# One-hot sort comparisons of a graph kernel, regrouped from alternating three-column units to whole pieces of six columns

## Chip, cores and metric

The kernel runs on one core of one Trainium2 chip. The metric is device time in microseconds (us) of one execution. The kernel before was run three times: 1296.0, 1299.63 and 1299.84 us, median 1299.63 us.

## What is computed

A residual graph layer on 6250 nodes and 206,250 edges of 128 float32 features. The edges' features are added up by the node that `src` names, the sum goes with `x` and one global vector through a small network, and the result is normalised:

```
edge_aggr = zeros((n, 128)).at[src].add(edge_attr_128)
combined = concat([x, edge_aggr, global_expand], -1) @ W_c + b_c
h = softplus(combined @ W1 + b1)
h = softplus(h @ W2 + b2)
x = layernorm(x + h @ W3 + b3)
```

Nearly all the time goes into the first line: the nodes are in no order that the core could use, so the kernel sorts the edges by node range itself.

## The kernel before, in words

The 6250 nodes are cut into 32 buckets of 196. The edges lie as 1692 columns of 122 edges, one edge per partition. Two columns make a pair (846 pairs), three pairs make a **piece** (`pieces`, L1094), and the pairs belong to eight groups of 28 to 128 pairs. A group whose number of pairs is no multiple of three ends in a smaller piece.

Five kinds of work run at once through one long stretch, each on an engine of its own:

- **Positions** (L445 to L760, VectorE with small matmuls on TensorE): for each coming group, in which place of a column each edge lands when the column is sorted by bucket (`slot`), and where the sorted pairs go in memory (`pair`). The tiles `pair_ib`, `past`, `hi_of` and `sum_of` belong to it. Groups 5 to 7 go through the counting twice; their first passes are laid into the time of groups 2 to 4.
- **Comparison** (`compare`, L1124): for each column a one-hot matrix `sort_hot`, 122 edges by 128 places, which says where each edge goes. VectorE does it by one equality of `slot` with a row of numbers. ScalarE does it in two steps: per column an `Abs` of the difference (L1140, the column's `slot` being its bias operand), then one `Relu` of 1 minus that (L1142), whose bias operand is a column of the tile `ones`.
- **Gather** (`gather`, L1145, TensorE): one float32 matmul per column, one-hot by edge rows, into a PSUM bank of a pool of three. The profile counts each such matmul twice.
- **Settle** (`settle`, L1157, ScalarE): two copies per three columns from the bank into one of six `pairs` tiles (sets 108 to 113), one tile for each piece.
- **Scatter** (`scatter_row`, L1176, GpSimd): one indirect DMA per pair writes its 128 rows to scratch memory (`rows_by`), 846 in all.

Rows that have been scattered are loaded back as `chunks` (L920), compared with the node numbers of a bucket on VectorE (`match`, tile `hot`, L983), multiplied on TensorE (`product`, L1006) and added up on VectorE (`add`, tile `sums_t`, L1029). What is still left of these sums when the last pair has been scattered is done together with the node network (`node_layers`, L1334), which ends the kernel. ScalarE also writes the bucket codes behind each load of edge rows (`code_rows`, L1105), and `log1p` (L1359) is a step of the softplus.

**Units before.** A piece of three pairs is two units of three columns (`units`, L1117), first the columns of even number (n = 0), then the odd ones (n = 1). By `(2 * i + n) % SHARE` with `SHARE` 2, each piece has its even unit compared on VectorE and its odd unit on ScalarE, there as three `Abs` and one `Relu` in a row. The comparison of a unit has a tile of its own, from a pool of five.

**What sets the order.** TensorE, VectorE, ScalarE and SyncE carry out their instructions in an order written by hand. Every step is entered with a planned time (`when`, L1248), all are sorted by it (L1325) and issued in that order; the planned times do nothing else. A scatter is planned every `SCATTER` = 1.3 us. With t the planned time of a piece's first scatter, its even unit is compared at t - 17.5, gathered at t - 14.0, settled at t - 10.5; its odd unit comes 1.95 us later in each (L1264 to L1266).

Of the kernel before, what the change touches and what calls it, by code (L numbers as in the profile page):

```python
# [7 lines left out]
F32 = mybir.dt.float32  # L8
# [5 lines left out]
AF = mybir.ActivationFunctionType  # L14
ALU = mybir.AluOpType
# [3 lines left out]
P = 128  # L19
# [18 lines left out]
PN = 122  # L38
# [4 lines left out]
PAIRS = 3  # L43
THREE = 3
# [15 lines left out]
SCATTER = 1.3  # L60
LOADED, CODED, COMPARED, GATHERED, SETTLED = 36.0, 21.0, 17.5, 14.0, 10.5
FIRST = 24.0
SOON, FLAGGED = 4.0, 15.9
SHARE = 2
PREP, LAG = 0.85, 11.0
TOGETHER, BEHIND = 2, 1
AT_END, FIRST_STEPS = 4, 9
# [74 lines left out]
def kernel(  # L142
# [21 lines left out]
    nc = tc.nc  # L164
# [15 lines left out]
    groups = []  # L180
# [74 lines left out]
    ones = const.tile([P, P], F32, name="ones")  # L255
# [57 lines left out]

    with ExitStack() as phase:
        rows_p = phase.enter_context(tc.tile_pool(name="rows", bufs=ROWS))
        sort_p = phase.enter_context(tc.tile_pool(name="sort", bufs=5))
        pairs_in = phase.enter_context(tc.tile_pool(name="pairs_in", bufs=2))
        per = phase.enter_context(tc.tile_pool(name="per", bufs=2))
        keep = phase.enter_context(tc.tile_pool(name="keep", bufs=1))
# [3 lines left out]
        iota_ps, slot_ps, twice_ps = (both_ps[:, a:a + w] for a, w in (  # L323
            (0, BL), (2 * P, P), (3 * P, P // 2)))
# [8 lines left out]
        dump, by_slot, bucket_of, quad_of, twice, half_p, before_f, awaited = (  # L333
            of_plain[n] for n in ("dump", "by_slot", "bucket_of", "quad_of", "twice", "half_p",
                                  "before", "awaited"))
# [106 lines left out]
        slot_of, pair_of, ends_of = {}, {}, ([0.0, 0.0], [0.0, 0.0])  # L442
        slots_done, pairs_done = set(), set()
# [615 lines left out]
        def node_rows():  # L1059
# [16 lines left out]
            def biases():  # L1076
# [17 lines left out]
        pieces = [(g, t, min(PAIRS, s1 - t)) for g, (s0, s1) in enumerate(groups)  # L1094
                  for t in range(s0, s1, PAIRS)]
# [9 lines left out]
        def code_rows(i):  # L1105
            a, b = LOAD_COLS * i, min(LOAD_COLS * (i + 1), NC)
            nc.scalar.copy(rows_at[i][:PN, :b - a, D:W], pair_low[:, a:b].unsqueeze(2))  # L1107
# [9 lines left out]
        def units(i):  # L1117

            k = pieces[i][2]
            return [(i, lo, min(THREE, k - lo), n) for lo in range(0, k, THREE) for n in range(2)]  # L1120

        hot_of, sorted_of = {}, {}

        def compare(unit):  # L1124
            i, lo, m, n = unit
            g, c, _ = pieces[i]
            slot = slot_of[g]
            assert all((g, 2 * (c - groups[g][0] + lo + j) + n) in slots_done for j in range(m))
            hot = sort_p.tile([P, THREE, P], F32, name="sort_hot")
            hot_of[unit] = hot  # L1130
            if (2 * i + n) % SHARE == 0:
                at = 2 * (c - groups[g][0] + lo) + n
                nc.vector.tensor_tensor(  # L1133
                    hot[:PN, :m],
                    slot[:PN, at:at + 2 * m - 1:2].unsqueeze(2).to_broadcast([PN, m, P]),
                    slot_ps[:PN].unsqueeze(1).to_broadcast([PN, m, P]), op=ALU.is_equal)
                return
            for j in range(m):
                at = 2 * (c - groups[g][0] + lo + j) + n
                nc.scalar.activation(hot[:PN, j], by_slot[:PN], AF.Abs,  # L1140
                                     bias=slot[:PN, at:at + 1], scale=-1.0)
            nc.scalar.activation(hot[:PN, :m], hot[:PN, :m], AF.Relu, bias=ones[:PN, :1],  # L1142
                                 scale=-1.0)

        def gather(unit):  # L1145
            i, lo, m, n = unit
            hot = hot_of.pop(unit)
            out = opened_bank(lambda: settle(unit))
            sorted_of[unit] = out
            for j in range(m):  # L1150
                at = 2 * (lo + j) + n
                col = 2 * pieces[i][1] + at
                nc.tensor.matmul(out[:, j, :], hot[:PN, j],  # L1153
                                 rows_at[col // LOAD_COLS][:PN, col % LOAD_COLS, :],
                                 start=True, stop=True)

# [37 lines left out]
        with tc.manual_schedule(engines={ET.PE, ET.DVE, ET.Activation, ET.SP}):  # L1194
# [53 lines left out]
            def when(t, step):  # L1248
                events.append((t, len(events), step))
# [5 lines left out]
            for i, t in enumerate(first_at):  # L1255
                if t >= LOADED:
                    when(t - LOADED, lambda i=i: load_rows(i))
                when(t - CODED, lambda i=i: code_rows(i))
            for i, t in enumerate(begins):
                mine = units(i)  # L1260
                for u, unit in enumerate(mine):
                    late_by = SCATTER * pieces[i][2] * u / len(mine)
                    soon = 0.0 if i or u else SOON
                    when(t - COMPARED + late_by - soon, lambda unit=unit: compare(unit))  # L1264
                    when(t - GATHERED + late_by - 1.7 * soon, lambda unit=unit: gather(unit))
                    when(t - SETTLED + late_by, lambda unit=unit: settle(unit))  # L1266
            for t, i, j in at_time:
# [66 lines left out]
    def node_layers(sums, ready):  # L1334
# [23 lines left out]

        def log1p(layer, n0, w):  # L1359
            away = sub_z[layer, n0][1]  # L1360
            nc.scalar.activation(away[:, :w], away[:, :w], AF.Ln, bias=ones[:, :1])

        def softplus(layer, n0, w):

# [240 lines left out]
```

## Time and profile before

The profile is of one execution on the chip. That execution took 1298.25 us, of which the span from the first to the last instruction is 1296.5 us; 1.75 us lie around it. It is 1.38 us under the median of the three runs.

| | before |
|---|---|
| median of three runs | 1299.63 us |
| the profiled execution, and its span | 1298.25 us, 1296.5 us |
| TensorE matmuls busy | 1169.6 us (90%) |
| VectorE (DVE) busy | 1073.4 us (83%), 2403 instructions |
| ScalarE (ACT) busy | 1064.2 us (82%), 2484 instructions |
| GpSimd (POOL) busy | 877.7 us (68%), 915 instructions |
| mean granted TensorE clock | 0.963 |
| mean DMA traffic | 295 GB/s |
| first scatter, last scatter begin | 23.39 us, 1132.43 us |

The profile names PE (TensorE), DVE (VectorE), ACT (ScalarE), POOL (GpSimd) and SP (SyncE), and lines as L1140, the line of the program. A group's row gives the line, engine and operation, what is written and read, the number of instructions, then busy time and mean length of one, then the idle time of the engine just before them and what ended it. A timeline row gives start, length and instruction; its bracket is idle time before it with what ended that. In the chain of waits a row is a start, a duration and what the time went to. Two float32 instructions in a row can overlap at their ends, so several together can take less than their lengths added up.

### The profile page before, as it was taken

Reading aid. Unit: us, or ns where it says so; the run is one execution under the profiler, and the core shown is the slowest. Engines: PE = TensorE matmul, PEld = TensorE weight load, DVE = VectorE, ACT = ScalarE, POOL = GpSimd, SP = SyncE. Lnnn points to the kernel's source line nnn. Section 1 sums busy time; section 2 is a strip of 40 time slices with the busy share of each in tenths; the row PEclk is TensorE's granted clock in tenths of the full one; section 3 lists DMA queues with packets and bytes.
Section 4 is the critical chain, followed back from the end, with each engine's and each line's share of the span. In section 5 each row is a group of like instructions: output and inputs, shape, how many; then the busy total and the mean of one; then the engine's idle time right before and its main releaser. Section 6 shows DMA issues by size and latency. Waiting matters only on the chain.

```text
span 1296.5 us, 26618 instructions
## 1 busy us (share of the span) xinstructions
PE 1169.6 (90%) x8617; PEld 1108.0 (85%) x8617; DVE 1073.4 (83%) x2403; ACT 1064.2 (82%) x2484; POOL 877.7 (68%) x915
## 2 busy tenths in 40 slices
PE   5767898878999998999899999999999999999893
PEld 4657788877998898998799999999999999998762
DVE  7968988998899988899878887799877666687784
ACT  5998998899978898987999999998999999504353
POOL 2777777777776677776777777777777777740334
PEclk9888998989999899999999999999999999999996
DMA  6789998899999998996989999999999999874421
GB/s 227 245 273 346 344 326 305 305 337 369 364 321 316 362 329 295 311 316 238 314 296 306 325 332 321 355 294 325 337 348 336 361 340 353 279 220 144 142 77 52
DMA packets 174638, 381.99 MB, mean 295 GB/s; under 512 B 27546, under 2 KB 118626, under 8 KB 160670
## 3 DMA queue, kind: packets, MB, share of 16 engines
q1 hardware_dynamic: 130751, 260.70, 60.4%
q0 software_dynamic: 41328, 115.65, 23.0%
q10 hardware_dynamic: 2415, 3.87, 0.8%
q8 instruction: 72, 1.18, 0.4%
q14 instruction: 72, 0.59, 0.1%
HBM read 242.49 MB, written 142.20 MB: 297 GB/s over the span
## 4 chain that ended last, share of the span: by engine, by line
PE 42%; DVE 21%; DMA 15%; ACT 9%; issue 7%; POOL 6%; SPq 0%; ACTq 0%; DVEq 0%; POOLq 0%
PE part L1006 24%; PE sorted L1153 13%; DMA rows_by<-pairs,pair 11%; POOL rows_by L1182 6%; ACT pairs L1165 6%; DVE hot L983 4%; DMA chunks<-rows_by 3%; ACT sort_hot L1140 2%; DVE sort_hot L1133 2%; DVE pair_ib L491 2%; DVE past L720 2%; DVE sums_t L1029 2%; DVE slot L569 1%; PE small L1383 1%; DMA rows<-in_edge 1%
## 5 line engine op out<-in xcount | busy, mean ns | idle before, releaser
L1182 POOL DMA_INDIRECT rows_by<-pairs,pair x846 | 824.8, 975 | 306.9 <-issue 204.5
L1006 PE MATMUL part<-hot,chunks 128*128 128x196 f32 x3516 | 674.1, 335 | 12.2 <-DVE sums_t L1029 9.2
L1165 ACT COPY pairs<-sorted 64x387 f32<-64x387 f32 (+2 forms) x1144 | 542.7, 474 | 70.0 <-PE sorted L1153 49.5
L1006 PEld LDWEIGHTS part<-hot,chunks 128*128 128x128 f32 x3516 | 581.1, 192 | 21.2 <-DVE sums_t L1029 10.3
L1153 PE MATMUL sorted<-rows,sort_hot 122*128 122x129 f32 x3384 | 497.4, 287 | 43.3 <-ACT pairs L1165 37.2
L1153 PEld LDWEIGHTS sorted<-rows,sort_hot 122*128 122x128 f32 x3384 | 454.0, 198 | 55.6 <-ACT pairs L1165 51.8
L983 DVE TENSOR_TENSOR hot<-chunks,both_ps 128x784 f32<-128x784 f32 (+3 forms) x541 | 427.9, 810 | 5.6 <-DMA chunks<-rows_by 5.2
L1140 ACT ACTIVATE sort_hot<-plain,slot 122x128 f32<-122x128 f32 x846 | 278.3, 391 | 13.1 <-DVE slot L569 7.1
L1029 DVE TENSOR_TENSOR sums_t<-sums_t,part 128x392 f32<-128x392 f32 (+1 forms) x262 | 143.5, 548 | 117.4 <-PE part L1006 116.7
L1142 ACT ACTIVATE sort_hot<-sort_hot,ones 122x384 f32<-122x384 f32 (+2 forms) x286 | 174.6, 611 | 9.3
L1133 DVE TENSOR_TENSOR sort_hot<-slot,both_ps 122x384 f32<-122x384 f32 (+2 forms) x286 | 154.5, 541 | 3.2 <-PE sorted L1153 3.0
L491 DVE TENSOR_TENSOR pair_ib<-pair_block,both_ps 122x512 bf16<-122x512 bf16 (+2 forms) x157 | 103.5, 664 | 0.3
L1425 POOL TENSOR_SCALAR y<-y,mv,rs 128x128 f32<-128x128 f32 x40 | 31.1, 785 | 96.9 <-issue 67.7
L569 DVE TENSOR_REDUCE slot<-small 122x16 f32<-122x512 f32 (+2 forms) x109 | 72.8, 668 | 15.3 <-PE small L552 14.8
L1355 ACT ACTIVATE away<-sorted,z_bias 128x512 f32<-128x512 f32 (+2 forms) x13 | 8.5, 656 | 70.8 <-DMA chunks<-rows_by 46.3
L550 PE MATMUL small<-pair_ib,half 122*122 122x512 bf16 (+2 forms) x109 | 43.0, 395 | 10.0 <-DVE slot L569 9.6
L735 PEld LDWEIGHTS <-past 128*128 128x128 f16 x424 | 24.9, 99 | 17.9 <-DVE past L720 12.6
L720 DVE TENSOR_TENSOR past<-both_ps,starts 128x512 f16<-128x512 f32 (+1 forms) x61 | 40.0, 666 | 0.3
L735 PE MATMUL small<-jump,past 128*128 128x56 f16 (+3 forms) x424 | 29.2, 190 | 11.5 <-DVE past L720 8.1
L1107 ACT COPY rows<-pair_i 122x16 f32<-122x16 f32 x106 | 22.6, 213 | 17.8 <-DMA rows<-in_edge 16.9
L552 PEld LDWEIGHTS <-starts_h 128*122 128x122 bf16 x236 | 24.9, 146 | 12.1 <-issue 7.6
L720 DVE TENSOR_TENSOR past<-both_ps,starts_late 128x512 f16<-128x512 f32 (+2 forms) x49 | 32.3, 661 | 0.0
(163 smaller groups left out, 520.0 us busy)
## 6 DMA issues: line engine op xcount, KB each, us to landing
rows<-in_edge SPq DMA_DIRECT2D x105, 1032.0 KB
chunks<-rows_by SPq DMA_DIRECT2D x362, 136.0 KB
chunks<-rows_by SPq DMA_DIRECT2D x203, 204.0 KB
chunks<-rows_by SPq DMA_DIRECT2D x75, 272.0 KB
rows_by<-pairs,pair POOLq DMA_INDIRECT x846
rows_by<-fill SPq DMA_DIRECT2D x10, 1249.5 KB
rows_by<-fill SPq DMA_DIRECT2D x10, 714.0 KB
chunks<-rows_by SPq DMA_DIRECT2D x13, 408.0 KB
```

The source lines that it names most:

```text
L491: nc.vector.tensor_tensor(ib, pair_block[:, cols].unsqueeze(2).to_broadcast([PN, n, SB]), iota_ps[:PN, :SB].unsqueeze(1).to_broadcast([PN, ...
L569: nc.vector.tensor_reduce(to, of, axis=mybir.AxisListType.X, op=ALU.max)
L720: nc.vector.tensor_tensor(past[:, :, a:b], twice_ps[:KB].unsqueeze(1).unsqueeze(1).to_broadcast([KB, 2, b - a, P // 2]), own["starts"][:, ...
L983: nc.vector.tensor_tensor(hot[:, q - a:q - a + m], chunks[j][:, lo:hi + 1:step, D:W].to_broadcast([P, m, BL]), iota_ps.unsqueeze(1).to_bro ...
L1006: nc.tensor.matmul(part[:, b - base_of[v], :], t[:, place_in(j, q), :D], hot[:, q - a], start=first, stop=last)
L1029: nc.vector.tensor_add(here, here, of)
L1133: nc.vector.tensor_tensor(hot[:PN, :m], slot[:PN, at:at + 2 * m - 1:2].unsqueeze(2).to_broadcast([PN, m, P]), slot_ps[:PN].unsqueeze(1).to ...
L1140: nc.scalar.activation(hot[:PN, j], by_slot[:PN], AF.Abs, bias=slot[:PN, at:at + 1], scale=-1.0)
L1142: nc.scalar.activation(hot[:PN, :m], hot[:PN, :m], AF.Relu, bias=ones[:PN, :1], scale=-1.0)
L1153: nc.tensor.matmul(out[:, j, :], hot[:PN, j], rows_at[col // LOAD_COLS][:PN, col % LOAD_COLS, :], start=True, stop=True)
L1165: nc.scalar.copy(sets_at[i][64 * n:64 * n + 64, lo:lo + m, h, :W], out[64 * h:64 * h + 64, :m, :])
L1182: s = nc.gpsimd.indirect_dma_start(out=dst, out_offset=bass.IndirectOffsetOnAxis(ap=at, axis=0), in_=rows[:, j].rearrange("p a b -> p (a b ...
```

## The change

`compare` works by piece. A piece of even number is compared whole on VectorE, in one instruction of six columns (122x768 for a full piece). A piece of odd number is compared whole on ScalarE: six `Abs`, one per column in column order, and one `Relu` over all six. `Relu` (and the `Ln` in `log1p`) gets its 1 as a number in the instruction instead of a column of `ones`. The tile pool `sort` has three tiles of six columns where it had five of three. The ScalarE steps of a piece are entered one by one, starting at t - 19.5 and 0.65 us apart (`SPREAD`, `SCATTER / 2`), so that the seventh, the `Relu`, has t - 15.6; the VectorE step stays at t - 17.5. Gathers, settles, scatters and all else keep their planned times.

```diff
-SHARE = 2
+SHARE, SPREAD = 2, 2.0
...
-        sort_p = phase.enter_context(tc.tile_pool(name="sort", bufs=5))
+        sort_p = phase.enter_context(tc.tile_pool(name="sort", bufs=3))
...
-            hot = sort_p.tile([P, THREE, P], F32, name="sort_hot")
-            hot_of[unit] = hot
-            if (2 * i + n) % SHARE == 0:
...
-            nc.scalar.activation(hot[:PN, :m], hot[:PN, :m], AF.Relu, bias=ones[:PN, :1],
-                                 scale=-1.0)
+            hot = hot_of[i] = sort_p.tile([P, 2 * PAIRS, P], F32, name="sort_hot")
+            if i % SHARE == 0:
+                return [lambda: nc.vector.tensor_tensor(
+                    hot[:PN, :2 * m], slot[:PN, at:at + 2 * m].unsqueeze(2).to_broadcast([PN, 2 * m, P]),
+                    slot_ps[:PN].unsqueeze(1).to_broadcast([PN, 2 * m, P]), op=ALU.is_equal)]
+            return [lambda j=j: nc.scalar.activation(
+                hot[:PN, j], by_slot[:PN], AF.Abs, bias=slot[:PN, at + j:at + j + 1], scale=-1.0)
+                for j in range(2 * m)] + [lambda: nc.scalar.activation(
+                    hot[:PN, :2 * m], hot[:PN, :2 * m], AF.Relu, bias=1.0, scale=-1.0)]
...
-                nc.tensor.matmul(out[:, j, :], hot[:PN, j],
+                nc.tensor.matmul(out[:, j, :], hot[:PN, at],
...
+                if i % SHARE == 0:
+                    when(t - COMPARED - soon, lambda i=i: compare_next(i))
+                else:
+                    for j in range(2 * pieces[i][2] + 1):
+                        when(t - COMPARED - SPREAD + j * SCATTER / 2, lambda i=i: compare_next(i))
...
-                    when(t - COMPARED + late_by - soon, lambda unit=unit: compare(unit))
...
-            nc.scalar.activation(away[:, :w], away[:, :w], AF.Ln, bias=ones[:, :1])
+            nc.scalar.activation(away[:, :w], away[:, :w], AF.Ln, bias=1.0)
```

`compare_next(i)` issues the next of a piece's steps. What stands on TensorE, GpSimd and SyncE, and in which order, is the same as before. On VectorE and ScalarE it changes.

ScalarE in the second group, before: the copies of piece 28 (set 112, even number) and piece 29 (set 113, odd number) and what stands around them.

```order
L1140 ACTIVATE sort_hot<-plain,slot 122x128 x3
L1142 ACTIVATE sort_hot<-sort_hot,ones 122x384
L1165 COPY pairs_112<-sorted 64x3x129 x4
L1140 ACTIVATE sort_hot<-plain,slot 122x128 x3
L1142 ACTIVATE sort_hot<-sort_hot,ones 122x384
L1165 COPY pairs_113<-sorted 64x3x129 x4
```

ScalarE at the same place now, from the last `Abs` of piece 29 to the `Relu` of piece 31.

```order
L1133 ACTIVATE sort_hot<-plain,slot 122x128
L1135 ACTIVATE sort_hot<-sort_hot 122x768
L1158 COPY pairs_112<-sorted 64x3x129 x4
L1133 ACTIVATE sort_hot<-plain,slot 122x128 x2
L1158 COPY pairs_113<-sorted 64x3x129 x2
L1133 ACTIVATE sort_hot<-plain,slot 122x128 x3
L1158 COPY pairs_113<-sorted 64x3x129 x2
L1133 ACTIVATE sort_hot<-plain,slot 122x128
L1135 ACTIVATE sort_hot<-sort_hot 122x768
```

Six `Abs` of two runs of three stand now in runs of two, three and one, between the two pairs of copies of a ScalarE piece, and one `Relu` of 768 stands for two of 384.

VectorE in the fifth group (while pairs 348 to 471 are scattered), before, with the two comparisons of two neighbouring pieces:

```order
L983 TENSOR_TENSOR hot<-chunks,both_ps 128x784
L1133 TENSOR_TENSOR sort_hot<-slot,both_ps 122x384
L491 TENSOR_TENSOR pair_ib<-pair_block,both_ps 122x512
L720 TENSOR_TENSOR past<-both_ps,starts_late 128x512
L569 TENSOR_REDUCE slot<-small 122x2x2x4
L1029 TENSOR_TENSOR sums_t<-sums_t,part 128x392
L491 TENSOR_TENSOR pair_ib<-pair_block,both_ps 122x512
L1133 TENSOR_TENSOR sort_hot<-slot,both_ps 122x384
L720 TENSOR_TENSOR past<-both_ps,starts_late 128x512
L983 TENSOR_TENSOR hot<-chunks,both_ps 128x784 x2
```

VectorE at the same place now:

```order
L983 TENSOR_TENSOR hot<-chunks,both_ps 128x784
L491 TENSOR_TENSOR pair_ib<-pair_block,both_ps 122x512
L720 TENSOR_TENSOR past<-both_ps,starts_late 128x512
L569 TENSOR_REDUCE slot<-small 122x2x2x4
L1029 TENSOR_TENSOR sums_t<-sums_t,part 128x392
L491 TENSOR_TENSOR pair_ib<-pair_block,both_ps 122x512
L1130 TENSOR_TENSOR sort_hot<-slot,both_ps 122x768
L720 TENSOR_TENSOR past<-both_ps,starts_late 128x512
L983 TENSOR_TENSOR hot<-chunks,both_ps 128x784 x2
```

The comparison of the odd-numbered piece is gone from VectorE; that of the even-numbered one has twice the columns, at the place of its first unit.

VectorE at the start of the program, before, where the first pieces are compared between the position steps of the first group:

```order
L1133 TENSOR_TENSOR sort_hot<-slot,both_ps 122x384
L720 TENSOR_TENSOR past<-both_ps,starts 128x512
L569 TENSOR_REDUCE slot<-small 122x2x4
L720 TENSOR_TENSOR past<-both_ps,starts 128x2x128
L746 TENSOR_SCALAR hi_of<-small,plain 128x56
L751 TENSOR_TENSOR sum_of<-hi_of,small 64x28 x2
L757 TENSOR_SCALAR pair<-sum_of 128x28
L1133 TENSOR_TENSOR sort_hot<-slot,both_ps 122x384 x2
```

VectorE at the same place now:

```order
L1130 TENSOR_TENSOR sort_hot<-slot,both_ps 122x768
L720 TENSOR_TENSOR past<-both_ps,starts 128x512
L569 TENSOR_REDUCE slot<-small 122x2x4
L720 TENSOR_TENSOR past<-both_ps,starts 128x2x128
L746 TENSOR_SCALAR hi_of<-small,plain 128x56
L751 TENSOR_TENSOR sum_of<-hi_of,small 64x28 x2
L757 TENSOR_SCALAR pair<-sum_of 128x28
L1130 TENSOR_TENSOR sort_hot<-slot,both_ps 122x768
```

The first comparison, ahead of the `past` steps that lead to the first scatter's addresses, has six columns instead of three; the two of three columns behind the `pair` step (pieces 1 and 2) are one of six (piece 2), and piece 1 is compared on ScalarE.

More of the change, by code (lines that the diff above doesn't have):

```diff
@@ L1122, with compare @@
         hot_of, sorted_of = {}, {}
[L1124 to L1128, printed above, removed]
-            hot = sort_p.tile([P, THREE, P], F32, name="sort_hot")
-            hot_of[unit] = hot
-            if (2 * i + n) % SHARE == 0:
[L1132 to L1142, printed above, removed]
-                                 scale=-1.0)
+        def compare(i):
+            g, c, m = pieces[i]
+            slot, at = slot_of[g], 2 * (c - groups[g][0])
+            assert all((g, at + j) in slots_done for j in range(2 * m))
+            hot = hot_of[i] = sort_p.tile([P, 2 * PAIRS, P], F32, name="sort_hot")
[7 more added lines that the diff above has]
+                    hot[:PN, :2 * m], hot[:PN, :2 * m], AF.Relu, bias=1.0, scale=-1.0)]
         def gather(unit):
             i, lo, m, n = unit
-            hot = hot_of.pop(unit)
+            hot = hot_of[i]
             out = opened_bank(lambda: settle(unit))
@@ L1258, with compare_next @@
                 when(t - CODED, lambda i=i: code_rows(i))
+            comparing = {}
+            def compare_next(i):
+                if i not in comparing:
+                    comparing[i] = compare(i)
+                comparing[i].pop(0)()
             for i, t in enumerate(begins):
                 mine = units(i)
+                soon = 0.0 if i else SOON
+                if i % SHARE == 0:
[3 more added lines that the diff above has]
+                        when(t - COMPARED - SPREAD + j * SCATTER / 2, lambda i=i: compare_next(i))
                 for u, unit in enumerate(mine):
```

## The prediction

> **What bounds the kernel now.** I read the groups first, then GpSimd's timeline, the busy time by stage, the waits, and last the chain of waits. The largest group of GpSimd and its timeline in a late stage (start, length, idle before):
>
> ```profile
> L1182 POOL DMA_INDIRECT rows_by<-pairs,pair x846 | 824.8, 975 | 306.9 <-issue 204.5
> 23.39 1.22 POOL L1182 DMA_INDIRECT rows_by<-pairs,pair  x1 [21.76 <-DVE much L635]
> 1002.09 0.97 POOL L1182 DMA_INDIRECT rows_by<-pairs,pair  x1 [0.30 <-issue]
> 1132.43 0.97 POOL L1182 DMA_INDIRECT rows_by<-pairs,pair  x1 [0.30 <-issue]
> ```
>
> GpSimd looks 68% busy, but with nothing to wait for a scatter follows the last after 1.28 us (0.975 and 0.30 of issue). From the first to the last, 845 steps take 1109.0 us; at 1.277 us they would take 1079.1. So sorting could end at most 30 us earlier, and the scatters are the floor below it. Where the 30 us are lost shows in POOL's busy time by stage (columns: length, then PE, PEld, DVE, ACT and POOL busy with counts, clock, DMA share, GB/s):
>
> ```profile
> 100.00:200.00 100.00, 83.37 (x689) 77.08 (x688) 88.37 (x216) 92.06 (x218) 75.14 (x77) 0.95 0.93 340
> 200.00:300.00 100.00, 85.93 (x692) 79.92 (x692) 91.23 (x238) 89.01 (x211) 74.99 (x78) 0.93 0.89 316
> 300.00:400.00 100.00, 92.27 (x713) 88.69 (x714) 87.72 (x205) 86.40 (x206) 71.05 (x74) 0.97 0.98 347
> 400.00:500.00 100.00, 89.44 (x696) 85.59 (x696) 89.44 (x219) 88.08 (x210) 71.67 (x74) 0.96 0.93 333
> 500.00:600.00 100.00, 95.42 (x745) 93.26 (x745) 91.36 (x215) 86.92 (x205) 71.54 (x75) 0.97 0.87 299
> 700.00:800.00 100.00, 100.00 (x762) 98.42 (x760) 85.41 (x167) 91.33 (x217) 75.41 (x78) 1.00 0.93 325
> 1000.00:1100.00 100.00, 99.16 (x699) 97.88 (x698) 68.20 (x105) 96.48 (x228) 76.20 (x79) 1.00 0.99 352
> ```
>
> 76.2 us per 100 is the full pace. Against it, (76.2 - busy)/76.2 of each stage is lost: 1.4 and 1.6 us in the two from 100 to 300, 6.8, 5.9 and 6.1 us in the three from 300 to 600; the other 8 of the 30 us lie before 100 and from 600 on, 1.0 of them in the stage from 700. Three causes stand behind it. Early, TensorE waits for ScalarE to empty banks (waits from 40 to 200):
>
> ```profile
> PEld sorted L1153 <- ACT pairs L1165: 24.2, 24, 1.9
> ACT pairs L1165 <- PE sorted L1153: 6.8, 4, 4.2
> ```
>
> ScalarE is the slower of the two there (24.2 us against 6.8), so it sets how far the sorted pairs get ahead of GpSimd. Second, DMAs that land late: from 300 to 400 they are 98% busy, and ScalarE waits for loaded rows with its copies behind the wait:
>
> ```profile
> 426.92 0.22 ACT L1107 COPY rows<-pair_i 122x16 f32<-122x16 f32 x1 [3.51 <-DMA rows<-in_edge]
> 430.92 1.01 POOL L1182 DMA_INDIRECT rows_by<-pairs,pair  x1 [3.59 <-ACT pairs L1165]
> ```
>
> Third, VectorE. The chain of waits runs through it without a break from 406 to 437, 441 to 474 and 561 to 621 us, 31 + 33 + 60 = 124 us; first and last rows, and a few of its steps:
>
> ```profile
> 406.46 0.56 DVE sums_t L1029
> 436.47 0.89 DVE hot L983
> ...
> 441.69 0.96 DVE hot L983
> 474.46 0.48 DVE sort_hot L1133
> ...
> 561.04 0.53 DVE sums_t L1029
> 585.89 0.88 DVE hot L983
> 586.77 0.47 DVE sort_hot L1133
> 620.21 0.61 DVE slot L569
> ```
>
> From 700 on TensorE is full too, but it has the same instructions in the same order as before. An earlier start of that stretch shifts it whole, with GpSimd at its pace beside it.
>
> **VectorE's part.** A full pair of pieces loses two comparisons of 384 elements and gets one of 768. By length:
>
> ```profile
> L1133 DVE TENSOR_TENSOR sort_hot<-slot,both_ps 122x384 f32<-122x384 f32 x279 | 152.3, 547 | 3.2 <-PE sorted L1153 3.0
> L983 DVE TENSOR_TENSOR hot<-chunks,both_ps 128x784 f32<-128x784 f32 x230 | 218.9, 963 | 5.3 <-DMA chunks<-rows_by 5.0
> ```
>
> 784 elements cost 963 ns, at (963 - 547)/400 = 1.04 ns each, so 768 cost 946, and 2 x 547 - 946 = 148 ns go. In the chain, where neighbours overlap, the steps are 0.47 and 0.88 us, so 2 x 0.47 - 0.87 = 0.07 us. VectorE's critical stretches run overlapped, so I take 0.07 and keep 0.15 as the far end. A pair of pieces is six scatters, 7.66 us; 124 us hold 16 pairs, which gives 1.1 us (up to 2.4).
>
> **ScalarE's part.** Its rows for the two operations, and two operations of one size, of which the first has a column as bias and the second has none:
>
> ```profile
> L1140 ACT ACTIVATE sort_hot<-plain,slot 122x128 f32<-122x128 f32 x846 | 278.3, 391 | 13.1 <-DVE slot L569 7.1
> L1142 ACT ACTIVATE sort_hot<-sort_hot,ones 122x384 f32<-122x384 f32 x279 | 171.6, 615 | 9.0
> L1142 ACT ACTIVATE sort_hot<-sort_hot,ones 122x128 f32<-122x128 f32 x5 | 2.0, 401 | 0.2
> L1361 ACT ACTIVATE away<-away,ones 128x512 f32<-128x512 f32 x22 | 15.9, 722 | 0.7
> L1356 ACT ACTIVATE away<-away 128x512 f32<-128x512 f32 x22 | 13.9, 630 | 0.7
> ```
>
> A Relu costs (615 - 401)/2 = 107 ns per 128 columns; the number instead of a column saves 722 - 630 = 92 ns. One Relu of 768 is then 615 + 3 x 107 - 92 = 844 ns for 2 x 615 = 1230: 386 ns less. [...]
>
> The Abs give something back. Where ScalarE runs without a break, three of them take 0.99 us:
>
> ```profile
> 333.94 1.96 ACT L1165 COPY pairs<-sorted 64x387 f32<-64x387 f32 x4
> 335.93 0.99 ACT L1140 ACTIVATE sort_hot<-plain,slot 122x128 f32<-122x128 f32 x3
> 337.59 1.96 ACT L1165 COPY pairs<-sorted 64x387 f32<-64x387 f32 x4
> ```
>
> That is 0.33 each, against 0.39 alone. Runs of two, three and one for two of three break one overlap and add small gaps: about 0.1 us. Net 0.28 us per pair of pieces (0.2 to 0.39), 40 us of ScalarE's busy time over 141 pairs. At full speed it needs 337.59 - 333.94 = 3.65 us for a piece whose scatters take 3.83; it gains 0.18 us of lead per piece now and would gain 0.32.
>
> What of it lies on the path: of the 3.0 us lost from 100 to 300, where ScalarE sets the lead, a lead that grows nearly twice as fast should remove two thirds, 2.0 us (0 to 3). In the catch-up stretches between 300 and 440, where ScalarE ran full for some nine pieces in my count of its timeline, 9 x 0.14 = 1.3 us. The DMAs' lateness itself stays. Lead at the entry of VectorE's stretches, and the waits before 100 and after 600: 1.3 us (0 to 4).
>
> **The edges.** At the start VectorE is on the path to the first scatter, and its first comparison is now 0.4 us longer (946 - 547 ns) ahead of the `past` step: +0.4 us. At the end three `Ln` stand in the chain (first and last below), 92 ns less each: -0.3 us.
>
> ```profile
> 1268.60 0.50 ACT away L1361
> ...
> 1280.48 0.61 ACT away L1361
> ```
>
> The pool of three tiles holds pieces, so VectorE's comparison waits for the gather of three pieces earlier, as far back as before; ScalarE's first Abs stands behind that piece's copies already. Both cost nothing.
>
> **Sum.** +0.4 - 1.1 - 2.0 - 1.3 - 1.3 - 0.3 = -5.6 us. From the profiled execution's 1298.25 us (span 1296.5 and 1.75 around it) that is 1292.7, and from the median, which is 1.4 us above it, 1294.0; I put 1293. Less than 0.3% (3.9 us) around the median, 1295.7 to 1303.5, can't be told from no change.
>
> **Rivals.**
>
> *The stalls come from elsewhere.* ScalarE's busy time falls by 40 us, but GpSimd loses its time to VectorE's stretches and to DMAs, and the quicker Relu ends in longer waits for TensorE. For it: in the stages from 300 to 600 ScalarE is under 89% busy. Left are +0.4 - 1.1 - 0.3 = -1.0: 1297 to 1299.
>
> *Much more goes.* Lead is capped by the six sets; if it stays near the cap up to 400, the 3.0 us and most of the 6.8 go, and the later stretches start with 4 or 5 us more: -15 us, 1283. The floor is 1298 - 30 = 1268. Against it: DMA share 0.98.
>
> *Slower: one Relu for six columns.* Before, the even unit of every piece came from VectorE. Now a ScalarE piece's first gather waits for the Relu, and that stands behind copies which wait for TensorE. Chain from the end of a ScalarE piece's odd gather: two copies 0.97, Abs 0.39, Relu 0.84, handovers 0.1, 2.3 us. Meanwhile TensorE has the two units of the piece between:
>
> ```profile
> 694.39 1.34 PE sorted L1153 x12
> 695.73 1.33 PE part L1006 x8
> ```
>
> With a product of 1.33 us between them the chain is nearly covered, with two it is; without one TensorE stands 2.3 - 1.34 = 0.96 us. By my count of its order 12 of 142 places are that short or nearly. If all twelve fell where GpSimd has no lead: +11.5 - 1.0, 1309 us; from six such places on (6 x 0.96 - 1.0 = 4.8) it is slower than can be missed. Against it: at most of them a lead should cover 1 us. That ScalarE keeps its order shows in the row at 426.92: three Abs that needed no loaded row started only behind the copy that did. [...]
>
> **Chances.** The forecast's own case, -4 to -12 us, 0.45; much more 0.10; stalls from elsewhere 0.33; slower 0.12. So faster 0.55, same 0.33, slower 0.12. The range 1285 to 1304 takes in the forecast's case with its bounds and the case of no change, and leaves out most of the other two.
>
> **What would show it.** Relu of 768 near 0.84 us, ScalarE's busy time down by about 40 us and VectorE's by 10 to 20; POOL busy above 75.5 per 100 us from 100 to 300, TensorE's waits for copies there below 24 us; 71 to 72 still in the three stages to 600. Wrong, if POOL's pace is unchanged up to 300, if waits of `sorted` for `sort_hot` on ScalarE appear by more than 5 us, or if the first scatter moves by over 1 us.

## The result and the profile after

The changed kernel took 1294.2 us (median of 8 runs, 1291.5 to 1296.98); the kernel before, run beside it, 1298.91 us (8 runs, 1296.0 to 1300.37). The ratio is 0.9966, 95% interval 0.9951 to 0.9981. That is 4.7 us less: faster, by more than 0.3% only just, and inside the forecast's range. The profiled execution of the changed kernel was the longest of its eight, 1296.98 us (span 1295.2), so its totals understate the change; a second profile, below, is of 1293.19 us.

The changed instructions, by group (busy time and mean ns of one, then idle before):

```profile
L1175 POOL DMA_INDIRECT rows_by<-pairs,pair x846 | 825.4, 976 | 307.1 <-issue 205.3 <-ACT pairs L1158 36.9 <-DMA rows_by<-pairs,pair 26.6
L1133 ACT ACTIVATE sort_hot<-plain,slot 122x128 f32<-122x128 f32 x840 | 292.8, 394 | 20.7 <-PE sorted L1146 7.3 <-DVE slot L569 7.0
L1130 DVE TENSOR_TENSOR sort_hot<-slot,both_ps 122x768 f32<-122x768 f32 x141 | 133.4, 946 | 1.5 <-PE sorted L1146 1.3
L1135 ACT ACTIVATE sort_hot<-sort_hot 122x768 f32<-122x768 f32 x138 | 116.3, 843 | 3.9
L1366 ACT ACTIVATE away<-away 128x512 f32<-128x512 f32 x22 | 13.9, 630 | 0.7
```

The lengths of single instructions came as forecast: the Relu of six 843 ns (forecast 844), VectorE's comparison 946 ns (946), the `Ln` 630 ns, 92 less than with a column. A scatter still costs 976 ns. VectorE is busy for 1063.8 us, 9.6 less; ScalarE for 1004.9 us, 59.3 less. The stages (length, PE, PEld, DVE, ACT and POOL busy with counts, clock, DMA share, GB/s) and the two ends of the scatters:

```profile
100.00:200.00 100.00, 85.80 (x690) 80.62 (x690) 86.89 (x202) 86.50 (x204) 76.19 (x79) 0.91 0.93 340
200.00:300.00 100.00, 83.97 (x672) 79.13 (x673) 88.11 (x216) 82.41 (x193) 73.53 (x76) 0.91 0.87 309
300.00:400.00 100.00, 92.42 (x720) 88.53 (x721) 86.59 (x197) 80.87 (x191) 69.72 (x72) 0.98 0.98 346
400.00:500.00 100.00, 87.45 (x696) 84.11 (x695) 89.11 (x208) 83.10 (x197) 72.29 (x75) 0.97 0.93 335
500.00:600.00 100.00, 95.40 (x731) 93.27 (x732) 90.17 (x203) 81.30 (x190) 72.58 (x75) 0.97 0.85 295
```

```profile
23.75 1.22 POOL L1175 DMA_INDIRECT rows_by<-pairs,pair  x1 [22.11 <-DVE much L635]
1133.15 0.97 POOL L1175 DMA_INDIRECT rows_by<-pairs,pair  x1 [0.30 <-issue]
```

From 100 to 200 GpSimd is now at its full pace (76.2); from 200 to 300 one stall of 3.1 us at 233 costs it that again; from 300 to 600 it has 214.6 us against 214.3. And a new wait is there. TensorE's and ScalarE's waits for each other from 40 to 200 (us in total, times, longest):

```profile
PEld sorted L1146 <- ACT sort_hot L1135: 16.5, 10, 2.4
PE sorted L1146 <- ACT sort_hot L1135: 14.9, 10, 2.2
ACT pairs L1158 <- PE sorted L1146: 11.3, 12, 4.7
PEld sorted L1146 <- ACT pairs L1158: 3.2, 9, 1.0
```

TensorE waited 24.2 us for ScalarE's copies there; now it waits 3.2 for them and 16.5 for the one Relu. The wait of the third rival is real, 22 places in the whole run and up to 2.2 us each. Whether it costs the end anything is what e4 and e6 below are for.

### The profile page after: what moved, and what is told of

It reads as the page before. It is cut to its first block, busy times and chain, and to the rows that moved or that the text cites. A ratio compares the mean times of both kernels' runs of the same rounds, so it can differ in the third digit from the quotient of the medians.

```text
span 1295.2 us, 26304 instructions
## 1 busy us (share of the span) xinstructions
PE 1171.1 (90%) x8617; PEld 1113.4 (86%) x8617; DVE 1063.8 (82%) x2260; ACT 1004.9 (78%) x2335; POOL 878.3 (68%) x915
## 4 chain that ended last, share of the span: by engine, by line
PE 59%; DVE 19%; DMA 10%; ACT 5%; issue 4%; POOL 3%; DVEq 0%; ACTq 0%; POOLq 0%; SPq 0%
PE part L1006 34%; PE sorted L1146 19%; DMA rows_by<-pairs,pair 5%; DVE hot L983 4%; DMA chunks<-rows_by 3%; POOL rows_by L1175 3%; ACT pairs L1158 2%; DVE past L720 2%; DVE sort_hot L1130 2%; DVE pair_ib L491 2%; ACT sort_hot L1133 1%; DVE sums_t L1029 1%; DVE slot L569 1%; PE small L550 1%; PE small L552 1%
## 5 line engine op out<-in xcount | busy, mean ns | idle before, releaser
L1006 PE MATMUL part<-hot,chunks 128*128 128x196 f32 x3516 | 675.9, 336 | 13.0 <-DVE sums_t L1029 9.4
L1158 ACT COPY pairs<-sorted 64x387 f32<-64x387 f32 (+2 forms) x1144 | 543.5, 475 | 123.2 <-PE sorted L1146 103.9
L1006 PEld LDWEIGHTS part<-hot,chunks 128*128 128x128 f32 x3516 | 582.8, 193 | 21.4 <-DVE sums_t L1029 10.5
L1146 PE MATMUL sorted<-rows,sort_hot 122*128 122x129 f32 x3384 | 498.2, 287 | 41.7 <-ACT sort_hot L1135 28.4
L1133 ACT ACTIVATE sort_hot<-plain,slot 122x128 f32<-122x128 f32 x840 | 292.8, 394 | 20.7 <-PE sorted L1146 7.3
L1029 DVE TENSOR_TENSOR sums_t<-sums_t,part 128x392 f32<-128x392 f32 (+1 forms) x262 | 143.4, 547 | 119.2 <-PE part L1006 118.6
L1130 DVE TENSOR_TENSOR sort_hot<-slot,both_ps 122x768 f32<-122x768 f32 x143 | 134.5, 940 | 1.9 <-PE sorted L1146 1.8
L1135 ACT ACTIVATE sort_hot<-sort_hot 122x768 f32<-122x768 f32 x143 | 118.6, 830 | 3.9
```

The lines of the kernel that those rows point to most:

```text
L1006: nc.tensor.matmul(part[:, b - base_of[v], :], t[:, place_in(j, q), :D], hot[:, q - a], start=first, stop=last)
L1029: nc.vector.tensor_add(here, here, of)
L1130: return [lambda: nc.vector.tensor_tensor(hot[:PN, :2 * m], slot[:PN, at:at + 2 * m].unsqueeze(2).to_broadcast([PN, 2 * m, P]), slot_ps[:P ...
L1133: return [lambda j=j: nc.scalar.activation(hot[:PN, j], by_slot[:PN], AF.Abs, bias=slot[:PN, at + j:at + j + 1], scale=-1.0) for j in rang ...
L1135: for j in range(2 * m)] + [lambda: nc.scalar.activation(hot[:PN, :2 * m], hot[:PN, :2 * m], AF.Relu, bias=1.0, scale=-1.0)]
L1146: nc.tensor.matmul(out[:, j, :], hot[:PN, at], rows_at[col // LOAD_COLS][:PN, col % LOAD_COLS, :], start=True, stop=True)
```

## Experiments

**The theories.** *A, lead* (the forecast's own): less work on ScalarE lets the sorted pairs run ahead of GpSimd. *B, elsewhere*: the gain comes from VectorE, the tail or the TensorE clock. *C, order*: what counts is that the Abs now stand singly between the copies. *D, one Relu*: the wait that it makes gives a part back. The kernel before was run beside each group of four (medians 1299.22, 1299.43 and 1299.18 us), so ratios are compared; 0.001 is 1.3 us, and the intervals reach 0.0012 to 0.0023 to each side.

### e1_after_again: the changed kernel once more

> The changed kernel once more, to have it beside the others on one chip and to have a second profile of it. Theory A (less ScalarE time lets the sorted pairs run further ahead of GpSimd): 0.9966 of before, 1294 us, and in a profile nearer to the median than the first one (1296.98 us) the loss against GpSimd's full pace before 700 us is smaller than the 28 us of before by 2 to 5 us. Theory B (the gain lies elsewhere: in the tail behind the last scatter, or in a granted TensorE clock that is higher in some executions): the same ratio, but the last scatter begins as late as before, within 1 us of 1132.4.

Ratio 0.9969 (0.9957 to 0.9981), 1294.25 us. Its profile, of 1293.19 us, has no stall of 3 us at 233 (columns as before, GpSimd alone):

```profile
100.00:200.00 100.00, 76.22 (x79) 0.95 0.94 342
200.00:300.00 100.00, 75.87 (x79) 0.95 0.91 321
300.00:600.00 300.00, 214.10 (x220) 0.97 0.91 323
700.00:1000.00 300.00, 227.61 (x234) 1.00 0.96 330
```

By the starts of the scatters, over 1.277 us a step, 1.7 us are lost from 100 to 300 (4.0 before), 20.0 from 300 to 600 (19.3), 1.4 from 700 to 1000 (3.1). The result stands. The last scatter begins at 1129.33, 3.1 us sooner than before, which theory B had ruled out; in this profile the gain up to there lies in the lead of the first 300 us and in the late stage. Another 2.1 us of its 5.2 come behind the last scatter, where the first profile, whose last scatter was no sooner, had 2.0 too; the part on the edges below returns to them.

### e2_number_only and e9_number_again: the number alone

```diff
 (the kernel before)
-            nc.scalar.activation(hot[:PN, :m], hot[:PN, :m], AF.Relu, bias=ones[:PN, :1],
+            nc.scalar.activation(hot[:PN, :m], hot[:PN, :m], AF.Relu, bias=1.0,
...
-            nc.scalar.activation(away[:, :w], away[:, :w], AF.Ln, bias=ones[:, :1])
+            nc.scalar.activation(away[:, :w], away[:, :w], AF.Ln, bias=1.0)
```

> The kernel before with one part of the change alone: Relu and Ln take their 1 as a number. ScalarE is busy 286 x 0.092 + 24 x 0.092 = 28.5 us less, half of the 59.3 us of the whole change. Theory A: half the gain, 0.9983, 1296.7 us. Theory C (what counts is the order, copies between single Abs): no gain, 0.9997 (the Ln in the tail, 0.3 us). Theory B: 0.9995 to 1.0.

> The number alone in the kernel before, a second time, beside the next three on one chip: each of those differs from it by one step towards the changed kernel. It had 1291.4 us and a ratio of 0.9941 (0.9923 to 0.9959). If that stands (0.993 to 0.995, 1290 to 1293 us), regrouping gives back 2 to 3 us of what the number saves, and the three tell which part of it does. If it was luck of the draw, it comes to 0.996 to 0.998, and the two kernels can't be told apart.

0.9941 (0.9923 to 0.9959), 1291.44 us; the second time 0.9954 (0.9939 to 0.997), 1292.29 us. The Relu of three takes 523 ns, 92 less:

```profile
L1142 ACT ACTIVATE sort_hot<-sort_hot 122x384 f32<-122x384 f32 x279 | 145.9, 523 | 8.8
```

ScalarE is busy for 1036.1 us, 28.1 less. So the smallest part of the change gives 6 to 7.7 us by itself, at least as much as the whole, and what was meant as the change's main part must be worth nothing or less beside it. Theory A has support here: nothing but ScalarE's time was touched. A higher clock isn't enough to explain it: the mean granted clock is 0.9645 in the runs of e2 and 0.9625 in the 25 runs of before beside them, and along those 25 a thousandth more goes with 0.4 us less, so that would be 0.8 us.

### e5_ones: regrouping alone

```diff
 (the changed kernel)
-                    hot[:PN, :2 * m], hot[:PN, :2 * m], AF.Relu, bias=1.0, scale=-1.0)]
+                    hot[:PN, :2 * m], hot[:PN, :2 * m], AF.Relu, bias=ones[:PN, :1], scale=-1.0)]
...
-            nc.scalar.activation(away[:, :w], away[:, :w], AF.Ln, bias=1.0)
+            nc.scalar.activation(away[:, :w], away[:, :w], AF.Ln, bias=ones[:, :1])
```

> The change without the number: Relu and Ln take their 1 from the column of ones again. ScalarE gets 143 x 0.092 + 24 x 0.092 = 15.4 us of its 59.3 us back. Theory A: three quarters of the gain stay, 0.9975, 1295.7 us. Theory C: the gain stays but for the 0.3 us of the Ln, 0.9968. A Relu of 768 takes 0.843 + 0.092 = 0.935 us.

0.9975 (0.996 to 0.9989), 1295.59 us: 3.3 us less than before by this ratio, where the whole change has 4.4. The number, worth 6 to 7.7 us in the old layout, is worth about 1 in the new one, which by the intervals can't be told from nothing. The parts don't add up: one of them gives back what another saves.

### e3_no_spread, e4_early_relu and e6_split_relu: is it the order, or the wait for the Relu?

In the first, ScalarE's seven steps of a piece are entered at one planned time; in the second they begin 2 us earlier; in the third there are two Relu of three columns, each after its own three Abs.

```diff
 (e3)
-                        when(t - COMPARED - SPREAD + j * SCATTER / 2, lambda i=i: compare_next(i))
+                        when(t - COMPARED, lambda i=i: compare_next(i))
 (e4)
-SHARE, SPREAD = 2, 2.0
+SHARE, SPREAD = 2, 4.0
 (e6)
+            steps = []
+            for n in range(2):
+                steps += [lambda j=j: nc.scalar.activation(
+                    hot[:PN, j], by_slot[:PN], AF.Abs, bias=slot[:PN, at + j:at + j + 1], scale=-1.0)
+                    for j in range(n, 2 * m, 2)]
+                steps.append(lambda n=n: nc.scalar.activation(
+                    hot[:PN, n:2 * m:2], hot[:PN, n:2 * m:2], AF.Relu, bias=1.0, scale=-1.0))
```

> The change without the spreading: the six Abs and the Relu of a ScalarE piece are entered together at 17.5 us ahead of its first scatter, so that 2.8 us of ScalarE stand in one block between copies; VectorE as in the change. ScalarE's time is that of the change or 0.1 us per two pieces less. Theory A: the whole gain stays, 0.9966 (0.9955 to 0.9975). Theory C: the gain is gone, copies wait up to 2.8 us, 1.000 (0.998 to 1.004). Theory D (the one Relu for both halves gives part of the gain back, 28 us of TensorE waiting for it): a Relu that is done about 1 us sooner in the order, waits for it at 10 to 20 us, 0.995 to 0.9966.

> The change with the ScalarE steps entered 2 us earlier (from t - 21.5 to a Relu at t - 17.6), still 0.65 us apart. Theory D: TensorE's waits for the Relu fall from 28 us to under 10 and the time falls by 1 to 4 us below the change, 0.993 to 0.996. Theory A: these waits were covered by the lead, or TensorE waits for copies instead; as the change, 0.9966 (within 0.001).

> The change with two Relu of three columns each for a ScalarE piece: the Abs of the even columns, their Relu, the Abs of the odd columns, their Relu. The first gather waits for the first Relu only, which stands about 2 us sooner in the order; ScalarE pays 141 x (2 x 0.523 - 0.843) = 29 us more. Theory D: TensorE's waits for the Relu fall below 10 us, and the time is at or below the change's, 0.995 to 0.9966. Theory A: half the gain is lost with the 29 us, 0.9983.

Ratios 0.9973 (0.996 to 0.9986), 0.9961 (0.9945 to 0.9977) and 0.996 (0.9944 to 0.9976). What TensorE waited for in e4, and in e6:

```profile
L1146 PE MATMUL sorted<-rows,sort_hot 122*128 122x129 f32 x3384 | 490.4, 285 | 34.1 <-ACT pairs L1158 23.9 <-DVE sort_hot L1130 9.5 <-issue 0.3
```

```profile
L1150 PE MATMUL sorted<-rows,sort_hot 122*128 122x129 f32 x3384 | 494.3, 286 | 39.0 <-ACT pairs L1162 31.3 <-DVE sort_hot L1130 7.2 <-issue 0.3
```

The 28.4 us of waits for the Relu are gone from both rows, and waits for copies stand in their place: 23.9 and 31.3 us, against 5.5 in the changed kernel. The time moves by some 0.8 us, less than the interval. So the new wait mostly replaced an old one: theory D is true of the trace, and nearly nothing of it reaches the end. Without the spread the Relu's wait goes too and 35.0 us of waits for copies come back, at 0.5 to 0.9 us worse by the ratios (1.4 by the medians of e3 and e1, taken on one chip), no clear difference either.

### e7_relu_one and e8_dve_twice: what an engine's microsecond is worth

In e7 the Relu covers one column of six, so the one-hot matrices of ScalarE's pieces are wrong in the others and the sums aren't the reference's; the order stays. In e8 VectorE's comparison is issued twice.

```diff
 (e7)
-                    hot[:PN, :2 * m], hot[:PN, :2 * m], AF.Relu, bias=1.0, scale=-1.0)]
+                    hot[:PN, :1], hot[:PN, :1], AF.Relu, bias=1.0, scale=-1.0)]
 (e8)
-                return [lambda: nc.vector.tensor_tensor(
+                def twice():
+                    for _ in range(2):
+                        nc.vector.tensor_tensor(
...
+                return [twice]
```

> How much ScalarE's time is worth: the Relu covers one column of the six, the other five are left without it (the sums are then not those of the reference; no instruction's length or order hangs on the values). ScalarE is busy 141 x 5 x 0.107 = 75 us less than in the change. Theory A, at the change's own rate of 4.4 us for 59 us: 5.6 us below the change, 0.992. If ScalarE's time is worth nothing any more: 0.9966, as the change.

> How much VectorE's time is worth: each of its comparisons of six columns is done twice in a row, 143 x 0.87 = 124 us more of VectorE. The critical stretches of VectorE hold 16 of them (124 us of the chain before, 7.66 us each). If only those count: 16 x 0.87 = 14 us above the change, 1308 us, 1.007. If the lead is eaten from 150 to 650 us everywhere: 65 x 0.87 = 57 us above, 1.040. VectorE's saving in the change (0.07 us a pair of pieces) is then worth 14/124 to 57/124 of its 9.6 us busy, 1.1 to 4.4 us; the second would make it the whole gain.

```profile
L1135 ACT ACTIVATE sort_hot<-sort_hot 122x128 f32<-122x128 f32 x143 | 42.1, 294 | 0.0
```

```profile
L1132 DVE TENSOR_TENSOR sort_hot<-slot,both_ps 122x768 f32<-122x768 f32 x282 | 267.6, 949 | 5.1 <-PE sorted L1149 0.2
```

Other instructions kept their lengths in e7, with other values in the matrices: a scatter 974 ns against 976 in e1, a gather's matmul 286 against 285, a product's 335 and an `Abs` 394 in both.

With ScalarE at 915.3 us of busy time (1003.6 in e1) the ratio is 0.9922 (0.9899 to 0.9944): 88 us less are worth 6 us, 0.07 us each. In the old layout 28 us were worth 6 to 7.7. ScalarE's time has no fixed price; in the new layout more of the saved time ends in waits for TensorE (`pairs` for `sorted`: 103.9 us in the changed kernel, 186.6 in e7). VectorE's 130 us more cost 51 us (1.0361, 1.034 to 1.0381, against 0.9967): 0.39 us each. At that price, measured by adding time and not by saving it, the 9.6 us saved on VectorE would be worth up to 3.8.

### e10_by_piece_units and e11_halves_burst: which part gives back

Each is one step from the number alone towards the changed kernel. e10 alternates by piece and leaves all else: units of three columns, each at its old time. e11 joins VectorE's two comparisons as the change does, with ScalarE's halves still in a row at their old times (and in the tile pool of the change); VectorE's second half is thereby planned 1.95 us sooner.

```diff
 (e10, from the number alone)
-            if (2 * i + n) % SHARE == 0:
+            if i % SHARE == 0:
 (e11, from e6)
-                        when(t - COMPARED - SPREAD + (j - (j >= m)) * SCATTER / 2, lambda i=i: compare_next(i))
+                        when(t - COMPARED + (j > m) * SCATTER * m / 2, lambda i=i: compare_next(i))
```

> The number, and comparisons alternate by piece and no longer by half piece; each is still of three columns, at its old place. If alternating by piece is what gives back (both halves of a ScalarE piece then stand behind ScalarE's copies, where before the first half came from VectorE at once), 0.996 to 0.998, 1294 to 1297 us, with TensorE's waits for ScalarE's comparisons at 10 us or more. If it is VectorE's comparison of six or the spread, it stays at 0.993 to 0.995.

> The changed kernel, with ScalarE's comparisons in two halves (three Abs and a Relu of three columns) at the places that they had before: from the run that alternates by piece it differs by VectorE's one comparison of six columns alone, from the run with two Relu by the spread. VectorE then saves 9.6 us as in the changed kernel. By the price from doubling its comparisons (0.4 us for each us) it should be up to 4 us faster than the run that alternates by piece; if a VectorE operation twice as long holds up what stands behind it, as fast or slower, 0.996 to 0.998.

e10: 1.0005 (0.9988 to 1.0022), 1299.34 us. Alternating by piece takes back the whole of what the number gave, 6.6 us by the ratios, with no wait for ScalarE's comparison; that part of the expectation fell. e11: 0.9976 (0.9957 to 0.9996), 1296.45 us.

A part of the 6.6 us is at the start. ScalarE's copies of the first piece in e10, and in e9:

```profile
23.83 0.97 ACT L1165 COPY pairs<-sorted 64x387 f32<-64x387 f32 x2 [2.44 <-PE sorted L1153]
```

```profile
22.13 0.97 ACT L1165 COPY pairs<-sorted 64x387 f32<-64x387 f32 x2 [0.70 <-PE sorted L1153]
```

The second half of the first piece is compared on VectorE in e10, behind the positions of its group, and the first scatter starts at 25.11 instead of 23.40 us. With one comparison of six (e11, and the changed kernel) that is gone again: 23.64. The rest shows as lead and as later stalls. By 220 us, ScalarE had made so many copies of sorted pairs, first in the kernel before, then in e10, e9 and e7 (length, ACT busy with the count of copies, clock, DMA share, GB/s):

```profile
0.00:220.00 220.00, 99.68 (x210) 0.92 0.82 292
```

```profile
0.00:220.00 220.00, 98.71 (x208) 0.91 0.81 289
```

```profile
0.00:220.00 220.00, 101.08 (x213) 0.92 0.83 296
```

```profile
0.00:220.00 220.00, 103.39 (x218) 0.94 0.84 300
```

GpSimd had started 152 or 153 scatters in all four, so four copies more are three scatters of lead, 3.8 us. e10, whose number should have put it ahead, is behind even the kernel before, and loses 5.0 us to stalls from 200 to 300 (e9 0.3). How alternation may cost lead is seen in e10's ScalarE: it has no comparison in one piece and two in the next, 2 x (0.98 + 0.52) = 3.0 us beside 1.96 us of copies, 5.0 us of work while GpSimd takes 3.83.

```profile
182.46 0.97 ACT L1165 COPY pairs<-sorted 64x387 f32<-64x387 f32 x2 [1.03 <-PE sorted L1153]
184.96 0.97 ACT L1165 COPY pairs<-sorted 64x387 f32<-64x387 f32 x2 [1.52 <-PE sorted L1153]
185.83 0.99 ACT L1140 ACTIVATE sort_hot<-plain,slot 122x128 f32<-122x128 f32 x3
186.84 0.52 ACT L1142 ACTIVATE sort_hot<-sort_hot 122x384 f32<-122x384 f32 x1
...
188.49 0.98 ACT L1140 ACTIVATE sort_hot<-plain,slot 122x128 f32<-122x128 f32 x3
189.51 0.52 ACT L1142 ACTIVATE sort_hot<-sort_hot 122x384 f32<-122x384 f32 x1
190.06 2.96 ACT L1165 COPY pairs<-sorted 64x387 f32<-64x387 f32 x6
```

It idles 1.03 and 1.52 us for TensorE, then runs 27 us without a break. From 40 to 200 its copies waited for TensorE 13.8 us in 8 places, in e9 with nearly the same instructions 9.0 us in 4. That alternation costs this is shown by the runs; that the uneven load is the way is read from these rows only. A rival is left open: the granted clock is lower in e10's profile (0.90 and 0.91 in the stages 100 to 200 and 200 to 300, in e9 0.95 in both), and TensorE's slower work could itself cost lead. Over the twelve runs of each the mean clock is 0.9624 and 0.9657; along the twelve of e10 a thousandth goes with 0.6 us, so this would be some 2 of the 6.6 us, if the clock is a cause and no consequence.

### e12_number_spread: the number, and the Abs between the copies, in the old units

```diff
 (the number alone)
-                    when(t - COMPARED + late_by - soon, lambda unit=unit: compare(unit))
+                    if (2 * i + unit[3]) % SHARE == 0:
+                        when(t - COMPARED + late_by - soon, lambda unit=unit: compare_next(unit))
+                    else:
+                        for j in range(unit[2] + 1):
+                            when(t - COMPARED + late_by - SPREAD + j * SCATTER * 0.75,
+                                 lambda unit=unit: compare_next(unit))
```

> The number in the kernel before, with the three Abs and the Relu of each half piece entered 0.98 us apart, the first 2 us earlier; VectorE as before. If Abs between the copies let banks come free sooner (the order theory), it beats the number alone: 0.990 to 0.993, with TensorE's waits for ScalarE's copies (pairs) below those of the number alone. If spreading is worth nothing, as in the changed kernel, it equals the number alone, 0.993 to 0.995; if it delays the Relu, slower than that.

0.9934 (0.9911 to 0.9956), 1289.24 us (6 runs, 1287.04 to 1292.91): by median 3 us under the number alone on the same chip and, by the ratios, 4.2 us under the changed kernel, though the intervals overlap in both pairs (against e1 alone, 0.9957 and up, they just come apart). It has the lowest median of all runs here. TensorE's waits for the copies from 40 to 200, in e9, then in e12:

```profile
PEld sorted L1153 <- ACT pairs L1165: 23.3, 24, 1.8
PE sorted L1153 <- ACT pairs L1165: 18.7, 17, 1.6
```

```profile
PEld sorted L1154 <- ACT pairs L1166: 18.3, 27, 1.2
PE sorted L1154 <- ACT pairs L1166: 14.2, 25, 1.0
```

More waits, shorter ones, and a smaller sum. By 220 us 216 copies are made, and the scatters lose 19.9 us in all, the least of any profile (30.0 before, 26.7 in e1); but this profile is of the fastest of the six executions, with a mean clock of 0.970. The 846 Abs are busy for 311.1 us as a group instead of 278.2, as they overlap no longer with each other; they overlap with the copies instead, and ScalarE as a whole has 1037.2 us against 1035.0. So e12 speaks for theory C where the load is even already; the step itself isn't clear of the noise by the ratios.

## Why the prediction was right, and where it was not

The ladder, by ratios: number alone 0.9948 (mean of two), alternating by piece 1.0005, one comparison of six on VectorE 0.9976, spread 0.996, one Relu 0.9967 (mean of two). In us: -6.8, +7.4, -3.8, -2.1, +0.9, together -4.3. By its parts' intervals such a step is uncertain by some 0.0025, 3 us: the first two are clear of that, the third only just, the last two aren't.

- **What bounds it** held. Scatters kept their pace of 1.277 us, and in e1 and e7 to e12 the time goes with the scatters' losses and start. The mechanism for ScalarE, lead, fits too, but loosely: copies made by 220 us go 208, 210, 213, 216 in e10, before, e9 and e12, and the times 1299.3, 1299.2, 1292.3 and 1289.2. The others don't keep that order: 210 in e6 for 1295.6 us, 211 and 214 in the changed kernel's two profiles for 1294.2, 218 in e7 for 1290.7. That lead carries the gain is likely, not shown.
- **ScalarE's busy time.** Forecast -40 us. The Relu fell from 174.6 to 118.6 us and the Abs rose from 278.3 to 292.8, net -41.5, as worked out; the `Ln` give 2.4 more. Yet the busy time fell by 59.3. The Abs gave nothing back: 846 of 391 ns before and 840 of 394 ns after both add up to 331 us, and what they no longer overlap with each other they overlap with the copies between them. A group's busy time shows only the first. So the forecast's 0.1 us per pair of pieces for the Abs, 14 us in all, was not there, and the Relu's 56.0 and the `Ln`'s 2.4 make up nearly all of the 59.3.
- **ScalarE's -4.6 us**: the step that failed. It priced 0.28 us per pair of pieces as lead without asking in what order ScalarE gets its work. The number alone, 0.09 us per piece, gave 6 to 7.7 us, more than the three terms for the whole; alternating by piece, costed at nothing, took as much back. Why alternating costs so much stays open between the uneven load and the clock, as said under e10. That the sum came out near is luck: two unpriced sizes cancel. Nor did the gain fall where it was put: from 300 to 600 nothing moved (214.3 us of GpSimd before, 214.6 and 214.1 after), so the -1.3 for the catch-up and the lead meant for VectorE's stretches weren't there. From 100 to 300 the forecast -2.0 is -2.3 in e1, and in the first profile nothing, for the one stall at 233.
- **VectorE's -1.1 (up to 2.4).** e10 to e11 gives -3.8 us, of which 1.5 are the start (25.11 to 23.64); 2.3 are left, at the far end, with an uncertainty of some 3. Busy time fell by 9.6 us, 0.07 per pair as taken; but the price of 0.39 us each was measured over the whole, not in 124 us of critical stretches only: from 300 to 600 e10 and e11 lose 16.4 and 17.6 us, and what e11 saves is in the stage from 200 to 300 (5.0 to 0.9 us), in lead again.
- **The edges.** Start: forecast +0.4, measured +0.36 and +0.2. Tail: forecast -0.3, and it did not reach the end. From the end of the last product (L1006) to the end of the span there are 30.06 us before, 30.05 and 30.06 in e2 and e9, and 30.2 in both profiles of the changed kernel; the last `Ln` starts sooner behind that product (13.5 us instead of 14.05), but what follows takes longer by as much. After the last scatter come 162.05 and 161.97 us against 164.07, but 164.75 in e11 with the same instructions there; this difference lies in the products ahead of the last one, and no run here says what sets it.
- **Rivals "elsewhere" and "much more".** Nothing of the stalls from 300 to 400 went (7.0 us before, 8.9 and 6.6 after), against the second; e2 and e9, with ScalarE's time alone changed, speak against the first. The 2 us behind the last scatter, which both profiles of the change have, stand in no term of the forecast and in neither of these rivals.
- **Rival "slower".** That ScalarE keeps its order, which it builds on, shows in the profile before: the copy at 426.92 us waited 3.51 us for a load, and the three `Abs` behind it start at 427.03. Its wait came, in 22 places instead of 12 and up to 2.2 us instead of 0.96, and would have passed its mark of six places; it failed because the waits for copies that it replaced were as long (37.2 us before; 28.4 for the Relu and 5.5 for copies after). The rival stood beside the real danger, a piece's two halves on one engine, and e10, which pays for that with no wait for a comparison, speaks for another mechanism than the one it named.
- **The signs.** The Relu's length and TensorE's waits for copies came; ScalarE's busy time fell by 59.3 us instead of about 40, and VectorE's by 9.6, just short of 10 to 20; POOL above 75.5 from 100 to 300 came in e1 and in one of the two stages of the first profile. The forecast's own mark of "wrong", waits of `sorted` for `sort_hot` over 5 us, was met at 28.4 us, and misled: a wait counts only for what it adds to the one that stood there.

## What to carry to other kernels

Try the parts of a change by themselves: here one constant passed as a number gave 6 to 7.7 us, and the regrouping around it gave back some 2.5 us of that. Where one engine works for another that must not fall behind, ask what it is given in each short period and not only its total; here the same comparisons, all in one piece and none in the next, cost 7 us, and the uneven load is the likely reason. A new wait in the trace is a loss only by what it exceeds the wait that it replaces.

## What the runs showed of the hardware

The granted TensorE clock falls to half in the middle of busy stretches: in the first profile after it is 0.50 from 228 to 231, from 328 to 330 and from 502 to 504 us, with TensorE busy through all three. TensorE's rows ahead of the stall at 233:

```profile
222.38 1.55 PE L1006 MATMUL part<-hot,chunks 128*128 128x196 f32 x8
...
225.83 0.89 PE L1146 MATMUL sorted<-rows,sort_hot 122*128 122x129 f32 x6
227.86 0.59 PE L550 MATMUL small<-pair_ib,half 122*122 122x512 bf16 x1 [1.14 <-DVE slot L569]
228.24 0.63 PE L552 MATMUL small<-half,starts_h 128*122 128x128 bf16 x4
228.66 2.81 PE L1006 MATMUL part<-hot,chunks 128*128 128x196 f32 x8
```

```profile
222.00:227.00 5.00, 4.19 (x32) 1.00 1.05 389
227.00:231.00 4.00, 3.14 (x12) 0.60 0.50 188
231.00:235.00 4.00, 3.69 (x41) 0.97 0.56 120
```

After an idle time of 1.14 us the eight matmuls of a product take 2.81 us, where the same eight took 1.55 at 222.38, and the clock of the four microseconds from 227 is 0.60. In e12 nearly the same idle time before the same matmul is followed by a full clock (1.00 from 220 to 228 us):

```profile
222.30 0.38 PE L550 MATMUL small<-pair_ib,half 122*122 122x512 bf16 x1 [1.16 <-DVE slot L569]
222.51 0.39 PE L552 MATMUL small<-half,starts_h 128*122 128x128 bf16 x4
222.74 1.55 PE L1006 MATMUL part<-hot,chunks 128*128 128x196 f32 x8
```

So an idle time of that length (1.14 us there, 1.16 here) is not enough to tell the two apart, and no run here shows what makes the clock fall. The eight runs of the changed kernel differ with the clock: 1296.98 us at a mean granted clock of 0.960, 1296.03 and 1294.91 at 0.963, and 1291.5 to 1294.51 from 0.965 up. Which comes first, the clock or the stalls, these runs don't tell.
